# Seven block products for eight in q, k and v: pre-norm attention and a top-1 adapter with projections through DRAM and a list-scheduled order

## The chip, the core and the metric

The kernel runs on one core of a Trainium2 chip. Times are device microseconds of one execution of the whole program. The engines are TensorE (PE; PEld is its weight load), VectorE (DVE), ScalarE (ACT), GpSimd (POOL) and SyncE (SP), which here issues every DMA.

## What is computed

Four sequences of 1024 tokens by 1024 features, all fp32. Each goes through attention with 32 heads of 32 features and rotary positions, and then through a layer that adds, for each token, the low-rank adapter (rank 16) of the one expert of eight that scores highest.

```
h = layernorm(x)
q, k, v = h @ wq, h @ wk, h @ wv          # 1024 x 1024 each
q, k = rotary(q), rotary(k)
p = softmax(causal(q @ k.T / sqrt(32)))   # per head
x = x + (p @ v) @ wo
h = layernorm(x)
gate = one_hot(argmax(h @ route.T)) * max(h @ route.T)
x = x + sum_e gate[e] * (h @ A[e].T) @ Bw[e].T
```

## The kernel before, in words

**Units.** The work is cut into 32 units: sequence b (0 to 3) and group g of four heads (0 to 7). A unit's q, k and v are 128 features by 1024 tokens each.

**Preparation.** A sequence's x is loaded in eight tiles of 128 tokens (`load_x`), normalized on DVE (`find_moments`, `normalize`), transposed on PE (`transposed`, L194) and kept as `xnT`, two halves of 512 tokens.

**Projections.** `chain` (L326) makes one of q, k, v for one half of the tokens: eight matmuls of 128x512 (L337) that accumulate in one PSUM bank. ACT evicts the bank; q and k are then rotated by a shuffle and a sine product on DVE (L369, L371) and a cosine product and a sum on POOL (L370, L375), and stay in SBUF as `qT` and `kT`. A unit has six chains, 48 matmuls. v is turned in 32x32 blocks (L1105), stored to DRAM and loaded in another layout (`spread_values`).

**Attention.** Queries go in 16 tiles of 64. `score_round` (L417) makes one to four tiles of scores in a four-bank PSUM tile, 16 matmuls of 32x32 weights per tile (L430). ACT copies them to SBUF (L441), POOL masks the diagonal (L444), DVE finds the maxima (`find_tops`, L462, joined over partitions at L483), ACT exponentiates (L491) and DVE turns the probabilities in 32x32 blocks (L516). `value_pieces` (L612) multiplies them by v for eight tiles at once: per step of 64 keys, eight matmuls of up to 256 columns (L634). `scale_values` divides by the sums on DVE (L654), straight out of PSUM, and the result goes to DRAM. Nine of the units' half-blocks get their reciprocal sums by a PE transpose (L605), the others through DRAM.

**Output.** `finish_steps` (L717) takes a tile of 128 tokens: the projection by wo (L751, 16 matmuls, wo streamed in chunks of 256 KB), the sum with x (L757), a second norm, its transposes, routing (L773) and adapter (L812), and the store. For the last sequence wo stays in SBUF, and the part of the projection that doesn't need the last unit is done ahead.

**What sets the order.** An order written out by hand: `SLOTS` lists the rounds of a unit; between the rounds, `fill` and `do_some` put steps from a list of dense work (projections of the next unit, output tiles of the sequence before), woven by `weave`, `change_steps` and step costs. All engines then run their instructions in this program order.

Of the kernel before, what the change touches and what calls it, by code (L numbers as in the profile page):

```python
# [24 lines left out]

SLOTS = (
    ((7, 0, 512), (6, 0, 448)),
    ((5, 0, 384), (4, 0, 320), (3, 0, 256)),
    "second",
    ((2, 0, 192), (1, 0, 128), (0, 0, 64), (9, 0, 640)),  # L30
    ((15, 0, 1024),),
    ((14, 0, 960),),
    ((13, 0, 896),),
    ((12, 0, 832),),
    "first",
    ((11, 0, 768), (8, 0, 256)),
    ((10, 0, 704), (8, 256, 576)),
)


SHARE, VALUE_SHARE, EACH = 3600, 2600, 330

APART_BY = 3

LENGTHS = (4.4, 4.3, 2.6, 3.0, 4.3, 3.8, 3.8, 3.8, 2.8, 2.8, 3.3)


class Step:


    def __init__(self, run, cost=1.0, chunk=None):
        self.run, self.cost, self.chunk = run, cost, chunk


def weave(main, other):

    if not other:  # L60
        return list(main)
    out, taken = [], 0
    for n, step in enumerate(main):
        out.append(step)
        due = (n + 1) * len(other) // len(main)
        out += other[taken:due]
        taken = due
    return out + list(other[taken:])
# [3 lines left out]
def tile_preln_attn_then_top1_lora(  # L72
# [25 lines left out]
    NC = D // P  # L98
    NT = S // P
# [8 lines left out]
    COUNT = {"row": 5, "w": 2, "qkT": 4, "rope": 3, "vT": 1, "vals": 1}  # L108
    small = ctx.enter_context(tc.tile_pool(name="small", bufs=2))
    dram = ctx.enter_context(tc.tile_pool(name="dram", bufs=2, space=bass.MemoryType.DRAM))  # L110
    ps_s = ctx.enter_context(tc.tile_pool(name="ps_s", bufs=1, space=bass.MemoryType.PSUM))
    ps = ctx.enter_context(tc.tile_pool(name="ps", bufs=4, space=bass.MemoryType.PSUM))
    ctx.enter_context(tc.manual_schedule())

    def bank(shape, name):
        return ps.tile(shape, F32, tag="ps", name=name)

    def row(name):
        return big.tile([P, D], F32, tag="row", name=name, bufs=COUNT["row"])


    eye_sb = const.tile([P, P], F32, name="eye_sb")

    def load_x(b, t, tag="row"):
        xr = big.tile([P, D], F32, tag=tag, name=f"x_{b}_{t}", bufs=COUNT[tag])
        nc.sync.dma_start(xr, x[b, t * P : (t + 1) * P, :])
        return xr

    def load_head(n, tag):
        wt = big.tile([P, NC, P], F32, tag=tag, name=f"w{n}_0", bufs=COUNT[tag])  # L130
        nc.sync.dma_start(wt, {"q": wq, "k": wk, "v": wv}[n][:, :P].rearrange("(c p) n -> p c n", p=P))
        return wt


    x_first = [load_x(0, 0)]
    nc.sync.dma_start(eye_sb, eye)
    x_first.append(load_x(0, 1))
    w_first = {"q": load_head("q", "w")}
    x_first.append(load_x(0, 2))
    w_first["k"] = load_head("k", "w")  # L140
    x_first.append(load_x(0, 3))
    rot_sb = big.tile([P, P], F32, tag="rope", name="rot_sb", bufs=3)
    nc.sync.dma_start(rot_sb, rot)
    cos_sb = const.tile([P, S], F32, name="cos_sb")
    nc.sync.dma_start(cos_sb, cos)
    sin_sb = const.tile([P, S], F32, name="sin_sb")
    nc.sync.dma_start(sin_sb, sin)
    w_first["v"] = load_head("v", "vals")


    causal_sb = const.tile([P, SQ], F32, name="causal_sb")
    for i in range(P // SQ):
        half, odd = divmod(i, 2)
        nc.sync.dma_start(
            causal_sb[i * SQ : (i + 1) * SQ],
            causal[half * SQ : (half + 1) * SQ, odd * SQ : (odd + 1) * SQ],
        )
    both_sb = const.tile([P, 2, SQ], F32, name="both_sb")
    first_sb = const.tile([P, E], F32, name="first_sb")
    nc.sync.dma_start(first_sb, first)  # L160
    half_sb = const.tile([P, 1], F32, name="half_sb")
    nc.vector.memset(half_sb, -0.5)
    sign_sb = const.tile([P, 1], F32, name="sign_sb")
    rec_sb = const.tile([P, 2, SQ], F32, name="rec_sb")
    nc.vector.memset(rec_sb, 0.0)

    def sign_sines():

        nc.vector.tensor_reduce(sign_sb, rot_sb, AX.X, ALU.add, negate=True)
        nc.vector.tensor_scalar(sin_sb, sin_sb, sign_sb, None, ALU.mult)  # L170
        of_eye = eye_sb.rearrange("p (s c k) -> p s c k", c=2, k=SQ)
        nc.vector.tensor_tensor(both_sb, of_eye[:, :, 0], of_eye[:, :, 1], ALU.add)


    def find_moments(src, name):
        stats = small.tile([P, D // 512, nc.vector.BN_STATS_DIM], F32, tag="stats", name=f"st_{name}")
        for i in range(D // 512):
            nc.vector.bn_stats(stats[:, i, :], src[:, i * 512 : (i + 1) * 512])  # L178
        mv = small.tile([P, nc.vector.BN_AGGR_DIM], F32, tag="mv", name=f"mv_{name}", bufs=3)
        nc.vector.bn_aggr(mv, stats)  # L180
        ve = small.tile([P, 1], F32, tag="ve", name=f"ve_{name}")
        nc.vector.tensor_scalar(ve, mv[:, 1:2], EPS, None, ALU.add)
        rstd = small.tile([P, 1], F32, tag="rstd", name=f"rstd_{name}", bufs=3)
        nc.gpsimd.tensor_tensor(rstd, ve, half_sb, ALU.pow)
        return mv, rstd

    def normalize(dst, src, moments):
        mv, rstd = moments
        nc.vector.tensor_scalar(dst, src, mv[:, 0:1], rstd, ALU.subtract, ALU.mult)

    def layernorm(dst, src, name):
        normalize(dst, src, find_moments(src, name))

    def transposed(dst, src, name, scalar_only=False):  # L194

        pts = []
        for half in range(NC // 4):
            pt = bank([P, 4, P], f"pt_{name}_{half}")
            for i in range(4):
                c = 4 * half + i  # L200
                nc.tensor.transpose(pt[:, i, :], src[:, c * P : (c + 1) * P], eye_sb)  # L201
            pts.append(pt)
        nc.scalar.copy(dst[:, 0:4, :], pts[0])  # L203
        if scalar_only:
            nc.scalar.copy(dst[:, 4:8, :], pts[1])
        else:
            nc.vector.tensor_copy(dst[:, 4:8, :], pts[1])


    units = [(b, g) for b in range(B) for g in range(NG)]  # L210
    weights = {(0, n): wt for n, wt in w_first.items()}
    to_load = deque((u, n) for u in range(1, len(units)) for n in "qkv")

    def load_weights():
        if not to_load:
            return
        u, n = to_load.popleft()
        g = units[u][1]
        wt = big.tile([P, NC, P], F32, tag="w", name=f"w{n}_{u}", bufs=2)
        w = {"q": wq, "k": wk, "v": wv}[n]  # L220
        nc.sync.dma_start(wt, w[:, g * P : (g + 1) * P].rearrange("(c p) n -> p c n", p=P))
        weights[u, n] = wt

    xnTs, qTs, kTs, vTs = {}, {}, {}, {}


    postponed = []

    def do_postponed(cost):
        for item in list(postponed):  # L230
            item[0] -= cost
            if item[0] <= 0:
                postponed.remove(item)
                item[1]()

    class Two:


        def __init__(self, parts):
            self.parts = parts  # L240

        def __getitem__(self, key):
            rows, cols = key
            k, at = divmod(cols.start, HALF)
            return self.parts[k][rows, at : at + cols.stop - cols.start]

    class Norm:

        def __init__(self, b, after, homes={}):
            self.b, self.after, self.homes = b, after, homes
            self.found = self.scaled = 0
            self.x, self.moments = {}, {}

        def load(self, *tiles):  # L260
            u = self.b * NG
            for t in tiles:
                n = self.homes.get(t)
                if not n:
                    self.x[t] = load_x(self.b, t)
                    continue
                if n == "chunk":
                    self.x[t] = Two([])
                    for cols in (slice(0, HALF), slice(HALF, D)):
                        part = big.tile([P, HALF], F32, tag="chunk", name=f"x_{self.b}_{t}", bufs=4)  # L270
                        nc.sync.dma_start(part, x[self.b, t * P : (t + 1) * P, cols])
                        self.x[t].parts.append(part)
                    continue
                dsts = qTs if n == "q" else kTs
                if u not in dsts:
                    dsts[u] = big.tile([P, S], F32, tag="qkT", name=f"{n}T_{u}", bufs=4)
# [49 lines left out]
    def chain(u, n, tb, parts=False):  # L326
# [6 lines left out]
        def step(c):  # L333
# [10 lines left out]
            if c == NC - 1:  # L344
                finish()
# [52 lines left out]

# [822 lines left out]
```

## Time and profile before

| | us |
|---|---|
| median of 3 runs (lowest, highest) | 2712.2 (2709.39, 2714.22) |
| span of the profiled execution | 2709.0 |
| PE busy | 2664.0 |
| DVE busy | 2143.4 |
| ACT busy | 1723.6 |
| POOL busy | 601.9 |

The span runs from the first to the last instruction of the profiled execution, and the times of the runs take in what lies around it: the median is 3.2 us above the span. A unit takes 64 to 66 us in the first sequence, where there is no output projection yet, and 81.5 us later (distance between the first of the score rounds with 512 columns).

### The profile page before, as it was taken

Reading aid. Unit: us, or ns where it says so; the run is one execution under the profiler, and the core shown is the slowest. Engines: PE = TensorE matmul, PEld = TensorE weight load, DVE = VectorE, ACT = ScalarE, POOL = GpSimd, SP = SyncE. Lnnn points to the kernel's source line nnn. Section 1 sums busy time; section 2 is a strip of 40 time slices with the busy share of each in tenths; the row PEclk is TensorE's granted clock in tenths of the full one; section 3 lists DMA queues with packets and bytes.
Section 4 is the critical chain, followed back from the end, with each engine's and each line's share of the span. In section 5 each row is a group of like instructions: output and inputs, shape, how many; then the busy total and the mean of one; then the engine's idle time right before and its main releaser. Section 6 shows DMA issues by size and latency. Waiting matters only on the chain.

```text
span 2709.0 us, 84062 instructions
## 1 busy us (share of the span) xinstructions
PE 2664.0 (98%) x35108; PEld 1300.3 (48%) x35108; DVE 2143.4 (79%) x4256; ACT 1723.6 (64%) x4978; POOL 601.9 (22%) x845
## 2 busy tenths in 40 slices
PE   8999999999999999999999999999999999999998
PEld 5444444444444544545444445444544444544445
DVE  4899988887787787887777877888787777787555
ACT  2878777876666676665666666766566666666521
POOL 2222222222222222222122222222212222212000
PEclk9999999999999999999999999999999999999999
DMA  3222323226554455652555554574355555446421
GB/s 119 60 72 73 76 72 80 64 65 176 139 141 130 124 138 154 165 164 65 164 158 134 136 132 131 137 189 140 83 158 143 154 134 138 122 132 198 127 70 53
DMA packets 465900, 332.74 MB, mean 123 GB/s; under 512 B 160880, under 2 KB 382320, under 8 KB 465520
## 3 DMA queue, kind: packets, MB, share of 16 engines
q1 hardware_dynamic: 465520, 327.37, 44.3%
q8 instruction: 276, 4.52, 0.7%
q14 instruction: 104, 0.85, 0.1%
HBM read 277.01 MB, written 50.26 MB: 121 GB/s over the span
## 4 chain that ended last, share of the span: by engine, by line
PE 80%; DVE 13%; ACT 3%; DMA 1%; issue 1%; POOL 1%; SPq 1%; POOLq 0%; DVEq 0%; ACTq 0%
PE po L751 15%; PE pq L337 14%; PE pk L337 14%; PE pv L337 12%; PE s L430 11%; PE av L634 8%; DVE top L462 4%; DVE pr L516 4%; PE ph L773 2%; PE pf L812 2%; ACT pr L491 1%; DVE both L483 1%; ACT pr L441 1%; PE pt_f L201 1%; DVE st_a L178 1%
## 5 line engine op out<-in xcount | busy, mean ns | idle before, releaser
L491 ACT ACTIVATE pr<-pr,both 128x256 f32<-128x256 f32 (+15 forms) x2048 | 1044.4, 518 | 53.6 <-DVE both L483 53.6
L441 ACT COPY pr<-s 128x640 f32<-128x640 f32 (+14 forms) x544 | 525.2, 1017 | 660.2 <-PE s L430 659.6
L462 DVE TENSOR_REDUCE top<-pr 128x2 f32<-128x960 f32 (+15 forms) x768 | 650.7, 894 | 251.4 <-POOL pr L444 250.8
L516 DVE STREAM_TRANSPOSE pr<-pr 128x1024 f32<-128x1024 f32 (+11 forms) x768 | 664.7, 908 | 34.1 <-ACT pr L491 30.7
L444 POOL TENSOR_TENSOR pr<-pr,causal_sb 128x128 f32<-128x128 f32 x512 | 237.2, 470 | 1158.3 <-ACT pr L441 1149.8
L337 PE MATMUL pv<-xnT,wv 128*128 128x512 f32 x1024 | 486.3, 602 | 0.0
L337 PE MATMUL pq<-xnT,wq 128*128 128x512 f32 x1008 | 478.1, 602 | 0.2 <-ACT xnT L203 0.2
L337 PE MATMUL pk<-xnT,wk 128*128 128x512 f32 x1008 | 477.1, 602 | 0.4 <-ACT rawq L363 0.4
L430 PE MATMUL s<-kT,qT 32*32 32x256 f32 (+4 forms) x17408 | 394.0, 386 | 9.4 <-POOL pr L444 3.2
L491 ACT ACTIVATION_READ_ACCUMULATOR pr<-pr,both 128x1 f32 x2048 | 400.8, 196 | 0.0
L751 PE MATMUL po<-chunk,attn 128*128 128x512 f32 x736 | 380.0, 602 | 2.5 <-DMA chunk<-in_wo 2.5
L430 PEld LDWEIGHTS s<-kT,qT 32*32 32x32 f32 x17408 | 187.3, 103 | 267.5 <-issue 100.7
L337 PEld LDWEIGHTS pk<-xnT,wk 128*128 128x128 f32 x1008 | 181.2, 190 | 235.7 <-issue 234.5
L337 PEld LDWEIGHTS pq<-xnT,wq 128*128 128x128 f32 x1008 | 183.2, 191 | 226.8 <-issue 225.0
L337 PEld LDWEIGHTS pv<-xnT,wv 128*128 128x128 f32 x1024 | 185.6, 190 | 218.1 <-issue 216.6
L634 PE MATMUL av<-pr,vals 64*32 64x256 f32 (+3 forms) x12288 | 272.8, 319 | 4.2 <-DVE pr L516 4.1
L634 PEld LDWEIGHTS av<-pr,vals 64*32 64x32 f32 x12288 | 213.0, 106 | 112.7 <-issue 66.1
L483 DVE TENSOR_TENSOR both<-top 32x4 f32<-32x4 f32 (+3 forms) x1152 | 207.4, 180 | 23.8
L751 PEld LDWEIGHTS po<-chunk,attn 128*128 128x128 f32 x736 | 135.6, 190 | 167.2 <-issue 149.4
L654 DVE TENSOR_TENSOR at<-av,by 128x256 f32<-128x256 f32 x128 | 48.2, 418 | 107.2 <-PE av L634 60.4
L751 PE MATMUL po<-wo,attn 128*128 128x512 f32 x256 | 116.6, 596 | 0.0
L375 POOL TENSOR_TENSOR qT<-qT,swapq 128x512 f32<-128x512 f32 x64 | 82.5, 1289 | 141.4 <-DVE swapq L371 141.4
(89 smaller groups left out, 1558.4 us busy)
## 6 DMA issues: line engine op xcount, KB each, us to landing
chunk<-in_wo SPq DMA_DIRECT2D x368, 256.0 KB, 3.8
vals<-vd SPq DMA_DIRECT2D x256, 128.0 KB, 4.3
x<-in_x SPq DMA_DIRECT2D x56, 512.0 KB, 5.4
wq<-in_wq SPq DMA_DIRECT2D x32, 512.0 KB, 4.7
wk<-in_wk SPq DMA_DIRECT2D x32, 512.0 KB, 4.0
wv<-in_wv SPq DMA_DIRECT2D x32, 512.0 KB, 4.3
vd<-vT SPq DMA_DIRECT2D x128, 128.0 KB, 4.6
out_y<-x SPq DMA_DIRECT2D x32, 512.0 KB, 2.6
```

The source lines that it names most:

```text
L337: nc.tensor.matmul(at["p"], lhsT=wt[:, c, :], rhs=xnTs[b, tb][:, c, :], start=(c == 0), stop=(c == NC - 1),)
L375: nc.gpsimd.tensor_tensor(dst[:, cols], dst[:, cols], other, ALU.add)
L430: nc.tensor.matmul(sc[i * SQ : (i + 1) * SQ, h, at : at + w].rearrange("p (j k) -> p j k", k=SQ), lhsT=of_q[rows, 2 * t + half], rhs=of_k[ ...
L441: nc.scalar.copy(pr[:, :, k0 : k0 + w], sc[:, :, at : at + w])
L444: nc.gpsimd.tensor_tensor(diagonal, diagonal, causal_sb.unsqueeze(1).to_broadcast([P, HG, SQ]), ALU.add)
L462: nc.vector.tensor_reduce(top[:, k, h : h + step], places[u, t][:, h : h + step, :], AX.X, ALU.max, negate=True,)
L483: nc.vector.tensor_tensor(dst[rows], src[rows], src[other], op)
L491: nc.scalar.activation(pr[:, h, :], pr[:, h, :], AF.Exp, bias=tops[u, t][:, h : h + 1], accum_out=dens[u, t // QT][:, t % QT, h : h + 1],)
L516: nc.vector.transpose(pr, pr)
L634: nc.tensor.matmul(avs[half][h * HD : (h + 1) * HD, t0:, :], lhsT=v[rows, j, h * HD : (h + 1) * HD], rhs=rhs, start=(j == 0), stop=(j == n ...
L751: nc.tensor.matmul(st["po"], lhsT=lhsT, rhs=rhs, start=(c == start), stop=(c == stop))
L773: nc.tensor.matmul(ph, lhsT=st["ynT"][:, c, :], rhs=w[:, c - i * RA, :], start=(c == 0), stop=(c == NC - 1),)
```

## The change

The kernel is written anew around the same parts. What differs:

- **Products.** Two outputs are made together (q and k of one group; v of two groups). The normalized x is seen as blocks A11 to A22 (512 tokens by 512 features) and the two weight slices as B11 to B22. Seven products of four matmuls each take the place of eight (`group`), with sums of blocks of x (S1 to S4) and of weights (T1 to T4) as operands, and sums of the results on DVE, POOL and in PSUM. The first group of all (q, k of unit 0) is made in the plain way.
- **Where things lie.** The T blocks are made once, in the first sequence, and stored in DRAM (`combine`), later loaded (`fetch_blocks`). q and k go to DRAM after their rotation (`rotate`), v after its turning (`spread`), and attention loads them. The next sequence's x is prepared during this one: blocks and S sums are written to DRAM (`prepare`) and fetched at the change of sequence (`fetch_sequence`).
- **Attention by quads.** Rounds are one tile each for 15 to 8, then (7, 6), (5, 4), (3, 2, 1, 0). Probabilities are multiplied by v for four tiles at once (`apply_quad`, up to 128 columns); ACT evicts the result, POOL divides (`finish_block`).
- **Output.** `finish_tile` does the same steps; the last sequence's tiles start only when all of its units are done.
- **Order.** Each piece is a `Task` with an engine, a length, a position and predecessors. `Plan.order` runs a list schedule over these lengths (the free engine takes the ready task with the lowest position whose buffers are free), and the program is written in order of the planned starts.

```diff
-SLOTS = (
-    ((7, 0, 512), (6, 0, 448)),
...
+ROUNDS = ((15,), (14,), (13,), (12,), (11,), (10,), (9,), (8,), (7, 6), (5, 4), (3, 2, 1, 0))
...
+SIGNAL = {"PE": 0.35, "ACT": 0.3, "DVE": 0.3, "POOL": 0.3}
+DENSE = 0.859
...
+    def group(b, kind, g, pos, w):
...
+        p1 = product("A11", "B11", one, True, [], True)
+        s1 = copy_out(r1, one, factor, pos, p1, True)
+        p2 = product("A12", "B21", two, True, [p1], True)
...
+        c11 = add(
+            "DVE", 0.62, lambda: add_bank(r1, two, factor), pos - 100, [p2, s1], [r1, two]
+        )
+        outs[0, 0] = r1, c11
+        p6 = product("S2", "T2", one, False, [p2, s1])
+        s2 = copy_out(r2, one, 1.0, pos, p6, True)
+        p5 = product("S1", "T1", two2, True, [p6], True)
+        s5 = copy_out(r5, two2, 1.0, pos, p5, True)
+        p7 = product("S3", "T3", one, False, [p5, s2])
+        s3 = copy_out(r3, one, 1.0, pos, p7, True)
+        c22 = add(
+            "POOL",
...
+            lambda: nc.gpsimd.tensor_tensor(r3.tile, r3.tile, r5.tile, ALU.add),
...
+        p3 = product("S4", "B22", two2, False, [p7, s5])
...
+        p4 = product("A22", "T4", one, False, [p3, s3])
+        c21 = copy_out(r4, one, factor, pos, p4, True)
...
+    def rotate(u, which, tb, raw, pos, t):
...
+            nc.sync.dma_start(store[u][:, cols], raw.tile)
...
+    def attend(b, g):
...
+            lambda: nc.sync.dma_start(kt.tile, k_dram[u]),
...
+            [stored["k", u, 0], stored["k", u, 1]],
...
+    def apply_quad(u, quad, pos, pr, vt, loads, turned, of_blk):
...
+        nj = QUADS * (quad + 1)
...
+                                [of_h.ap[0], [pitch(quad), QUADS - t0], [1, SQ]],
...
+            nc.scalar.copy(dst, src)
...
+            nc.gpsimd.tensor_tensor(done.tile, done.tile, by.tile, ALU.mult)
...
+    for t in plan.order():
+        for buf in t.opens:
+            make(buf)
+        t.run()
```

## Prediction

> **What bounds the kernel now.** I read the page's busy times first, then the chain that ended last, then busy times by stretch, then the timeline of TensorE inside one stretch.
>
> ```profile
> PE 2664.0 (98%) x35108; PEld 1300.3 (48%) x35108; DVE 2143.4 (79%) x4256; ACT 1723.6 (64%) x4978; POOL 601.9 (22%) x845
> ```
> ```profile
> PE 80%; DVE 13%; ACT 3%; DMA 1%; issue 1%; POOL 1%; SPq 1%; POOLq 0%; DVEq 0%; ACTq 0%
> ```
> TensorE (PE) is idle for 45.0 of 2709.0 us, and 80% of the chain is its work. So what the change takes off PE counts in full, unless another engine or a wait comes up to it. The next engine is VectorE (DVE). Busy times by stretch (columns: stretch and length; PE, weight loads, DVE, ACT, POOL busy; granted clock; DMA share; GB/s):
>
> ```profile
> 0.00:60.00 60.00, 50.03 (x250) 34.57 (x251) 28.48 (x57) 12.93 (x22) 15.42 (x20) 1.00 0.43 134
> 60.00:150.00 90.00, 87.34 (x1326) 40.99 (x1326) 72.25 (x138) 64.64 (x192) 23.25 (x34) 0.98 0.22 53
> 150.00:600.00 450.00, 439.33 (x6885) 207.51 (x6873) 405.95 (x802) 357.76 (x1033) 121.66 (x171) 1.00 0.30 74
> 600.00:2400.00 1800.00, 1791.60 (x23730) 866.63 (x23727) 1437.34 (x2850) 1160.11 (x3367) 407.20 (x564) 1.00 0.52 140
> 2400.00:2487.00 87.00, 87.00 (x1129) 41.49 (x1128) 67.96 (x138) 57.10 (x164) 18.65 (x26) 1.00 0.47 129
> 2487.00:2709.00 222.00, 208.70 (x1846) 109.09 (x1817) 131.44 (x275) 71.08 (x201) 15.75 (x31) 1.00 0.33 103
> ```
> The reader is to see two regimes. In the first sequence (150 to 600) there is no output projection yet, DVE is busy 405.95 of 450 us (90%), and PE still idles only 10.7 us (2.4%). From 600 to 2400 DVE is at 80% and PE idles 8.4 us (0.5%). The granted clock is full almost throughout. Prices on PE come from its timeline (start, length, records; a step's price is the distance to the next start):
>
> ```profile
> 699.96 1.88 PE L337 MATMUL pk<-xnT,wk 128*128 128x512 f32 x4
> 701.68 1.02 PE L751 MATMUL po<-chunk,attn 128*128 128x512 f32 x2
> 702.53 1.88 PE L337 MATMUL pq<-xnT,wq 128*128 128x512 f32 x4
> ...
> 764.55 3.69 PE L634 MATMUL av<-pr,vals 64*32 64x256 f32 x128
> 768.16 2.84 PE L337 MATMUL pk<-xnT,wk 128*128 128x512 f32 x6
> 770.93 2.35 PE L634 MATMUL av<-pr,vals 64*32 64x256 f32 x128
> 773.22 1.12 PE L751 MATMUL po<-chunk,attn 128*128 128x512 f32 x2
> ...
> 778.70 1.91 PE L430 MATMUL s<-kT,qT 32*32 32x96 f32 x128
> 780.54 1.13 PE L751 MATMUL po<-chunk,attn 128*128 128x512 f32 x2
> ```
> One fp32 matmul is two records. From 699.96 to 702.53 there are three of 128x512: 0.857 us each.
>
> **The change, part by part (PE).**
>
> *Projections.* The program built from the changed kernel has 1,316 matmuls of 128x512 for q, k, v and 128 of 128x128 (first group, like 32 whole ones): 1,348, against 1,520 + 64/4 = 1,536 before. 188 x 0.857 = **-161 us**. That is certain as work: these matmuls lie on the chain (q, k, v are 14 + 14 + 12% of it).
>
> *Probabilities times values.* Before, a unit (four heads) has one piece of eight steps at 256 columns, 768.16 - 764.55 = 3.61 us, and two ramps from 256 to 32 columns, 2.29 us each: 8.19. After, the columns are the same but in quads: 24 steps of 128 columns and four ramps 128, 96, 64, 32. A step of 128 columns at half of 3.61/8 is 0.226; a quad ramp is the end of the old ramp, 2.29 less its first four steps (0.451 + 0.395 + 0.338 + 0.282) = 0.82. 24 x 0.226 + 4 x 0.82 = 8.70, and some 0.3 for three more entries: 9.0, +0.85 a unit, x 32 = **+27 us**. From below 0 (same columns). From above by the record rate of narrow tiles: the timeline has 128 records of narrow score tiles in 1.84 us, 14.4 ns each; three-tile rounds run at 16.5 ns (96 records in 1.58 us); 640 records x 16.5 = 10.6 us a unit: +76.
>
> On these narrow steps the rows show 14.4 ns per record, 29 ns per fp32 matmul. The Trainium skill ("TensorE: Matmul & The Clock Gate", section "Wait — 56ns, not 53.3ns?") says that start-to-start "never drops below ≈25 ns however small N is", which speaks against cutting the steps narrower. Taken per record, this would be an estimated 640 x 25 = 16 us a unit, +250 us in all, and the change would lose. The row contradicts that reading already (14.4 ns), and taken per fp32 matmul the rule asks 320 x 25 = 8 us, below what I price.
>
> *Scores.* Tile 8 is no longer split in two and each of the tiles 8 to 15 is a round by itself. The lone rounds fall by 0.05 us per 32 columns from 1.07 (512) to 0.92 (416); continued, 384, 352, 320 and 288 cost 0.87, 0.82, 0.77, 0.72. Against the mixed rounds of before (1.43, 1.43, 1.58, 1.84 in the timeline), I get -0.23 a unit, **-7 us** (bounds -15 to +10). The 36 transposes of sums (L605) go, at 0.93 us per eight as pt_f has them: **-4 us**. Switches between dense and narrow work cost PE as before: its order has 2,450 rows of equal instructions against 2,504. Sum of PE work: -161 + 27 - 7 - 4 = **-145 us** (bounds -180 to -79).
>
> **The other engines, which decide how much of it arrives.**
>
> *DVE.* Added: 94 sums out of PSUM at 0.685 (L757: 50.7 us for 74) = 64; two more rounds of joins a unit, 256 x 0.163 (L483) = 42; v turned in 128 pieces at 0.401 (L516, 128x256) = 51 in place of 38 (L1105); 24 block sums of the first sequence at 0.70 = 17. Removed: scaling at L654, 48, and copies at L207, 17. Net +71: 2214 us. About 123 of them fall into the last 222 us (131 before), so some 2,091 stand before those. *ACT*: 128 more evictions of 256 columns at 0.378 (L441) = 48, 47 more of 512 at 0.58 = 27, 28 transposed halves = 16, less a little: some 1,810 us. *POOL*: 64 + 47 + 48 + 40 new operations of 128x512 at 1.28 (L370): +250, 850 us. Neither comes near PE's 2,530; both are hidden beside it, and would cost their +86 and +250 only if PE had nothing else to do meanwhile.
>
> *DVE beside POOL.* The same sine product takes 0.69 us in the timeline where POOL rests and 814 ns in the mean:
>
> ```profile
> L371 DVE TENSOR_TENSOR swapk<-swapk,sin_sb 128x512 f32<-128x512 f32 x64 | 52.1, 814 | 2.2
> ```
> So 250 us more of POOL can stretch DVE. From below nothing (the two rarely meet), from above 18% of its tensor-tensor work; I take 2 to 4% of the whole.
>
> *DMA.* q and k go out and come back (+67 MB), combined weights are stored and reloaded (+42), the next sequence's blocks are written and fetched (+44): 327 becomes some 480 MB.
>
> ```profile
> q1 hardware_dynamic: 465520, 327.37, 44.3%
> ```
> By bytes that is 44.3% x 480/327 = 65% of the queues, less by packets, since the 128-byte pieces of v go. The mean bandwidth is hidden. The danger is order: SP issues 2,094 DMAs in one queue (1,627 before). New waits on it: a unit's k and q are loaded only when its group has been rotated on DVE and POOL and stored. Queued behind such a store or load stand weights, wo chunks and values, and PE's next group waits for those.
>
> **PE's waiting.** Now 45 us: 10 in the first 60, 2.7 to 150, 10.7 + 8.4 in the middle, 13.3 in the last 222. After: the start waits for DVE (51 us of norms, rotations and block sums before the first score's maximum, against some 40 us of PE): +8. The tail is eight whole tiles of 16 x 0.857 + 0.93 + 1.85 + 0.16 + 1.72 = 18.4 us behind a last unit of some 60, plus an end chain of 15: 222 us again, with a thinner last unit: +5. In the middle, DVE's 2,091 us in about 2,380 are 88%, near the 90% of the first sequence, where PE lost 2.4%. I take 2% of 2,330 = 47 where it is some 20 now: +27. Together **+40** (bounds -10, every wait hidden better, to +130, the first regime's loss doubled and the start's too).
>
> Sum: 2709 - 145 + 40 = 2604 on the profiled execution's span of 2709.0; the median of the runs is 3 us above that span: **2607 us**.
>
> **Rivals.**
> - *All of it arrives.* Projections of later units can run ahead, since q, k, v lie in DRAM, so PE always has something. For it: the 0.5% of 600 to 2400. Against it: DVE at 88% rather than 80%. 2709 - 145 + 3 = 2567.
> - *DVE becomes the bound.* It is stretched 6% by POOL (2,091 becomes 2,216) and fills at most the 91% it reached from 150 to 450 (136.7 and 136.4 us of two stretches of 150): 2,216/0.91 = 2,436, and 222 for the tail: 2658, with the 3: 2661. For it: 814 against 690 ns. Against it: transposes and reductions, most of DVE's work, stretch less.
> - *Slower: one landing exposed per group.* 47 groups of seven products each fetch their operands (seven, or four in the first sequence) through the one queue. If a late store ahead of them exposes one landing, 4 us (chunks and weights land in 3.8 to 4.7 us by the median of their issues), this is 47 x 4 = 188: 2567 + 188 = 2755. It decides from 145/47 = 3.1 us a group. For it: SP already waits 572 us in front of wo chunks behind PE. Against it: six weight buffers, some 20 us of PE work ahead.
> - *It doesn't do what it says.* Excluded for the products (the counts above); it could be that the projections are not what PE waits on, but PE is the chain.
>
> **How the numbers follow.** Forecast 2607 (2575 to 2640): 0.45. All arrives, 2567: 0.2. DVE bound, 2661: 0.17. Slower, 2755: 0.15; the remaining 0.03 lies about no change (0.2%, what a measurement can tell, is 5 us). Faster 0.82, same 0.03, slower 0.15. The range takes in the first three and the edge of no change, and leaves most of the slower case and a little below: 2552 to 2710.
>
> **What would show it.** Right: PE busy near 2,530 us at 97%, DVE near 2,210 to 2,280, 88% before the tail; 128-column steps of probabilities times values at 0.23 us; idle of PE spread, mostly behind DVE or ACT. Wrong: PE waiting for weight buffers or for k and q by DMA (slower rival); DVE over 91% in the middle with a sine product over 850 ns (DVE bound); value steps near 0.4 us; a long hole at the start or between sequences, which I priced at a few us.

## The result and the profile after

| | before | after |
|---|---|---|
| median (lowest to highest) | 2711.9 us (2709.4 to 2714.2) | 2829.4 us (2819.6 to 2838.8) |
| ratio, 95% interval | 1 | **1.0435** [1.0409, 1.046] |
| span of the profiled execution | 2709.0 | 2817.8 |
| PE busy; idle (span less busy) | 2664.0; 45.0 | 2598.9; 218.9 |
| mean granted clock | 0.998 | 0.976 |

The changed kernel is 4.35% slower. Forecast were 2607 us, 2552 to 2710. The page after, its busy times and its chain:

```profile
span 2817.8 us, 99968 instructions
...
PE 2598.9 (92%) x41960; PEld 1294.6 (46%) x41960; DVE 2281.6 (81%) x4570; ACT 1805.8 (64%) x5136; POOL 889.1 (32%) x1035
...
q1 hardware_dynamic: 398048, 477.62, 55.1%
q8 instruction: 329, 5.39, 0.8%
...
PE 45%; DVE 13%; issue 4%; ACT 1%; DMA 1%; POOL 0%; SPq 0%; POOLq 0%; DVEq 0%; ACTq 0%
```
The work went mostly as planned: PE's busy time fell by 65 us although its clock was lower. The other side is idle time, +174: -65 + 174 = +109, the whole change of the span. So the question is not what the products cost but why PE stands still. PE's waits after (columns: us in total, times, longest), and the one row put down to "issue" before:

```profile
PE av L1118 <- issue: 100.3, 52, 5.4
PE av L1118 <- DVE pr L1083: 32.5, 30, 4.1
PE s L967 <- issue: 19.5, 23, 2.5
PE s L967 <- ACT pr L998: 11.6, 12, 1.9
```
```profile
PE s L430 <- issue: 2.5, 2, 1.3
```
The largest cause is "issue": PE waits for nothing that the profile shows. Of the +174, "issue" makes +122, waits for DVE +39 and for ACT +15. Waits put down to DMA come to 1.9 us (wo and the adapter's weights); none is for k, q or v. Where the "issue" gaps lie is told by PE's timeline (start, length, records, the idle time before):

```profile
708.18 1.82 PE L1118 MATMUL av<-pr,val 64*32 64x128 f32 x128
709.93 1.12 PE L762 MATMUL pc_qk<-S,b_qk 128*128 128x512 f32 x2
...
752.47 2.98 PE L1118 MATMUL av<-pr,val 64*32 64x128 f32 x169
756.53 1.30 PE L1118 MATMUL av<-pr,val 64*32 64x128 f32 x87 [1.08 <-issue]
...
826.15 2.62 PE L1118 MATMUL av<-pr,val 64*32 64x128 f32 x169
831.50 2.17 PE L1118 MATMUL av<-pr,val 64*32 64x128 f32 x87 [2.73 <-issue]
```
Eight key steps (708.18 to 709.93) take 1.75 us, about as priced (1.81). But runs of 16 steps, 256 records, break off in the middle, between equal instructions whose operands were all there. Counted from the program's start, these breaks are multiples of some 127.5 records apart (127, 128, 255, 383, 510, 638 ...). A record is one weight load and one matmul, so 128 are 256 PE instructions; the instruction queue q8 moved 5.39 MB in 329 packets, 5.39/329 = 16 KB each, which for 256 instructions is 64 bytes an instruction. **PE has used up its block of instructions before the next one is there.** All breaks in the middle of a run, of values and of scores, sum to 107 us; before there were 2.5.

The trace's DMA records show the blocks themselves. PE's 84,311 instructions after (weight loads, matmuls and its sequencer's) are 329.3 blocks of 256, and q8 moved 329 packets; before, 70,694 are 276.1, and q8 moved 276. All 68 breaks end 1.14 to 1.62 us behind the landing of such a packet. "Issue" gaps that end this way sum to 113 us; the other 12 us are six gaps at the first record of a value run, with no packet landing in the 14 us before, and what ended those isn't shown. In 16 of the 68 breaks the packet set out only after PE had stopped, up to 1.9 us after; what held it back stays open.

The second thing to see is the clock, here behind such gaps (same stretch, the same eight records of 128x512 twice):

```profile
849.96 0.71 PE L967 MATMUL s<-k,q 32*32 32x64 f32 x36 [1.15 <-issue]
850.60 5.95 PE L762 MATMUL pa_qk<-S,T_qk 128*128 128x512 f32 x8
856.39 3.60 PE L762 MATMUL pc_qk<-S,T_qk 128*128 128x512 f32 x8
```
Right after two gaps (1.95 us for ACT at 847, 1.15 here) the eight take 5.95 us instead of 3.60. Around the gap of 2.73 us at 831 (shown above) the granted clock (third number from the right) falls to half (columns: stretch and length; PE, weight loads, DVE, ACT, POOL busy; clock; DMA share; GB/s):

```profile
827.00:831.20 4.20, 1.77 (x127) 1.52 (x110) 4.01 (x11) 2.57 (x10) 0.14 (x1) 1.00 0.91 262
831.30:834.60 3.30, 3.10 (x88) 2.53 (x88) 3.27 (x8) 0.37 (x1) 0.89 (x1) 0.50 0.07 14
834.70:838.00 3.30, 3.30 (x70) 1.50 (x69) 1.30 (x2) 0.49 (x1) 0.79 (x1) 1.00 0.20 63
```
Most low stretches are 3.4 us long, so that each loses 1.7 us, and most stand behind a gap of 2 us or more. Summed over the span, (1 - granted clock) x length is **66.6 us** after and 5.1 before; PE was at work in 56 and 5 of them. So PE's work at full clock is 2598.9 - 56 = 2543 against 2664.0 - 5 = 2659: **-116**. The budget: -116 of work, +51 of clock, +174 of waiting: +109.

### The profile page after: what moved, and what is told of

Its sections match the earlier page's. It is cut to its first block, busy times and chain, and to the rows that moved or that the text cites. A ratio compares the mean times of both kernels' runs of the same rounds, so it can differ in the third digit from the quotient of the medians.

```text
span 2817.8 us, 99968 instructions
## 1 busy us (share of the span) xinstructions
PE 2598.9 (92%) x41960; PEld 1294.6 (46%) x41960; DVE 2281.6 (81%) x4570; ACT 1805.8 (64%) x5136; POOL 889.1 (32%) x1035
## 3 DMA queue, kind: packets, MB, share of 16 engines
q1 hardware_dynamic: 398048, 477.62, 55.1%
q8 instruction: 329, 5.39, 0.8%
## 4 chain that ended last, share of the span: by engine, by line
PE 45%; DVE 13%; issue 4%; ACT 1%; DMA 1%; POOL 0%; SPq 0%; POOLq 0%; DVEq 0%; ACTq 0%
PE po L1305 12%; PE av L1118 7%; PE s L967 6%; PE pa_qk L762 5%; DVE top L1026 5%; PE pa_v L762 3%; PE pc_qk L762 3%; DVE pr L1083 3%; DVE both L879 2%; PE ph L1366 2%; PE pf L1434 2%; PE pc_v L762 2%; PE pb_qk L762 2%; PE pt_f L351 1%; PE pb_v L762 1%
## 5 line engine op out<-in xcount | busy, mean ns | idle before, releaser
L1059 ACT ACTIVATE pr<-pr,both 128x512 f32<-128x512 f32 (+15 forms) x2048 | 1045.1, 518 | 110.5 <-DVE both L879 110.0
L1026 DVE TENSOR_REDUCE top<-pr 128x2 f32<-128x1024 f32 (+15 forms) x768 | 655.7, 895 | 157.5 <-POOL pr L1004 155.1
L998 ACT COPY pr<-s 128x2048 f32<-128x2048 f32 (+15 forms) x512 | 530.0, 1067 | 287.8 <-PE s L967 280.0
L1083 DVE STREAM_TRANSPOSE pr<-pr 128x640 f32<-128x640 f32 (+11 forms) x768 | 666.6, 907 | 58.3 <-ACT pr L1059 53.4
L1305 PE MATMUL po<-wo,attn 128*128 128x512 f32 x1024 | 503.8, 616 | 6.6 <-issue 5.0
L1118 PE MATMUL av<-pr,val 64*32 64x128 f32 x20480 | 328.8, 267 | 137.1 <-issue 100.3
L967 PE MATMUL s<-k,q 32*32 32x512 f32 (+3 forms) x16384 | 395.3, 402 | 32.4 <-issue 19.5
L1118 PEld LDWEIGHTS av<-pr,val 64*32 64x32 f32 x20480 | 297.4, 109 | 249.5 <-issue 171.1
L879 DVE TENSOR_TENSOR both<-top 32x4 f32<-32x4 f32 (+2 forms) x1408 | 312.5, 222 | 28.2
L762 PE MATMUL pa_qk<-A,T_qk 128*128 128x512 f32 x440 | 212.0, 607 | 0.4 <-ACT r_qk L730 0.4
```

The costliest lines, as they stand in the source:

```text
L762: nc.tensor.matmul(at.tile, lhsT=buf.tile[:, c, :], rhs=act.tile[:, c, :], start=first_ and c == 0, stop=c == KC - 1, skip_group_check=not ...
L879: nc.vector.tensor_tensor(dst[r], src[r], src[o], op)
L967: nc.tensor.matmul(s.tile[i * SQ : (i + 1) * SQ, h, at : at + w].rearrange("p (j k) -> p j k", k=SQ), lhsT=of_q[r, 2 * (t % QUADS) + half] ...
L998: nc.scalar.copy(place(t), s.tile[:, :, at : at + w])
L1026: nc.vector.tensor_reduce(got["top"][:, k, h : h + step], place(t)[:, h : h + step, :], AX.X, ALU.max, negate=True,)
L1059: nc.scalar.activation(pr[:, h, :], pr[:, h, :], AF.Exp, bias=got["both"][:, k, h : h + 1], accum_out=den(blk)[:, t % 8, h : h + 1],)
```

## The experiments

Two theories. **F**: blocks of instructions come too slowly for runs of narrow matmuls, and this and the low clock behind the pauses make the loss. **D**: probabilities are late, because DVE has more to do than planned. For the kernels that follow, "pauses" are gaps put down to "issue" in the middle of a value or score run, "clock" is the sum above over the whole span, pauses included; "before" ran beside all of them at 2710.5 to 2713.1 us.

| kernel | us | ratio [95%] | PE busy | idle | pauses | clock |
|---|---|---|---|---|---|---|
| after | 2829.4 | 1.0435 [1.0409, 1.046] | 2598.9 | 219 | 107 | 67 |
| half the values (1) | 2699.4 | 0.9958 [0.9943, 0.9973] | 2556.1 | 137 | 11 | 65 |
| before, quads (2) | 2830.1 | 1.0445 [1.0429, 1.046] | 2710.8 | 117 | 79 | 18 |
| before, traffic (3) | 2744.9 | 1.0126 [1.0111, 1.0141] | 2673.9 | 68 | 1 | 12 |
| both (4) | 2880.6 | 1.0625 [1.0607, 1.0643] | 2731.6 | 149 | 83 | 37 |
| eighth product (6) | 2949.5 | 1.0887 [1.0853, 1.0921] | 2753.3 | 208 | 99 | 66 |
| planner's lengths (7) | 2867.1 | 1.0579 [1.0563, 1.0595] | 2601.4 | 261 | 94 | 107 |
| spread (8) | 2936.9 | 1.0844 [1.0825, 1.0862] | 2649.4 | 282 | 17 | 131 |
| gentle (9) | 2790.3 | 1.0288 [1.0267, 1.031] | 2599.7 | 188 | 47 | 63 |
| rests (10) | 2786.7 | 1.0275 [1.0256, 1.0294] | 2598.8 | 190 | 48 | 59 |
| longer (11) | 2844.4 | 1.0481 [1.0459, 1.0503] | 2604.7 | 238 | 33 | 97 |
| one join, half the values (12) | 2610.4 | 0.9617 [0.9601, 0.9633] | 2533.2 | 83 | 4 | 43 |
| one join (13) | 2751.7 | 1.0152 [1.0137, 1.0167] | 2583.0 | 174 | 101 | 55 |
| rests, copies on DVE (14) | 2704.8 | 0.9972 [0.996, 0.9983] | 2579.0 | 122 | 32 | 29 |
| **rests, copies on POOL (15)** | **2666.9** | **0.9828** [0.9811, 0.9844] | 2576.8 | 95 | 43 | 34 |
| copies on POOL alone (16) | 2762.1 | 1.0185 [1.0164, 1.0207] | 2583.3 | 175 | 110 | 58 |
| before, copies on DVE (17) | 2695.6 | 0.9939 [0.9924, 0.9954] | 2660.9 | 33 | 0 | 3 |
| before, copies on POOL (18) | 2699.5 | 0.9954 [0.9939, 0.9969] | 2660.0 | 41 | 4 | 2 |

### F: what the pauses are

**1. Half the values.** In `apply_quad` of the changed kernel:

```diff
-                    for half in range(2):
+                    for half in range(2 if j == 0 else 1):
...
-                            stop=(j == nj - 1),
+                            stop=(j == nj - 1 or half == 1),
```


> The changed kernel, in which the second half of the queries gets only the first key step of probabilities times values (it leaves out nearly half of these matmuls; each step still streams 128 columns, so PE's streaming time stays). Theory F (PE runs out of instructions: it is refilled in blocks of 256 and stands still at a block's end): the pauses inside value runs go, some 100 us of PE idle, and the granted clock rises from 0.976 towards 0.99; 2690 to 2730 us. Rival D (an order planned on too short DVE lengths, so PE waits for DVE and ACT): same as the changed kernel within 30 us, 2800 to 2830.

2699.4 us, 130 less than after, of which only 40 are work at full clock. The pauses fall from 107 to 11 us. So most of what the runs of narrow matmuls cost is not their work. The clock did not recover (65), though F had expected that it would; waits of 33 us for DVE's transposes (33 before the edit) and 22 for ACT's copies (12) left gaps that lower it.

**2. The value edit in the kernel before.** Eight-tile steps of up to 256 columns cut into two of up to 128 (scalings doubled for it), nothing else of the change:

```diff
-                for h in range(HG):
-                    for half in range(2):
...
+                for lo, hi in ((t0, QT // 2), (max(t0, QT // 2), QT)):
...
+                    for h in range(HG):
+                        for half in range(2):
```


> The kernel before with one part of the change alone: each step of probabilities times values in two matmuls of up to 128 columns instead of one of 256 (and two narrow scalings more per half). F: pauses inside value runs appear in a kernel that had none, at distances of whole blocks of 256 instructions; idle +40 to +120 us, 2770 to 2850 us. Rival W (quads cost only their width and entries, as priced): 2735 to 2750, no pauses. D says nothing of it: 2712 to 2750.

2830.1: this edit alone costs +4.45%, as much as the whole change. PE's waits now begin with a line that the kernel before did not have:

```profile
PE av L640 <- issue: 76.9, 52, 3.3
PE pt_a L201 <- DVE x L189: 8.9, 2, 7.7
PE av L640 <- DVE pr L516: 6.3, 7, 2.7
```
All 76.9 us lie in the middle of runs, at the same distances as after, in a kernel without products of seven and without a planner, and all its 55 pauses (scores included) end 1.23 to 1.64 us behind the landing of a q8 packet. PE's busy time rose by 47 us, of which 12 are clock: the value steps were priced at +27.

**3 and 4. Traffic.** 488 copies of 256 KB from DRAM to DRAM, one behind each chunk load, in the kernel before (3) and together with the value edit (4):

```diff
+    def spare_copy():
+        k = copies[0] % 8
+        copies[0] += 1
+        sink = dram.tile([P, 512], F32, tag="sink", name=f"sink_{copies[0]}", bufs=8)
+        nc.sync.dma_start(sink, wo[k * P : (k + 1) * P, :512])
...
+        spare_copy()
```


> The kernel before with a copy from DRAM to DRAM of 256 KB behind each chunk load (488 copies, about 125 MB, near the traffic that the change adds); no other work. If a busier DMA makes the refill slower (theory T beside F): pauses on PE appear in value and score runs, 2725 to 2790 us. If traffic as such is harmless: 2707 to 2720.

> The kernel before with both the value steps by 128 columns and the added copies in DRAM, that is, two earlier edits together. If the pauses at block ends depend only on how fast the instructions are used up, the two costs add: some 2865 us, with pauses of about 1.5 us on average as with the value edit alone. If the traffic makes the fetching of blocks slower as well, the pauses grow and the time is 2880 to 2930 us.

(3) costs 33 us and has no pauses (1 us): its time lies in the range of slower fetching, but for another reason, waits for wo chunks, which grow from 2.5 to 28 us. (4) is 2880.6 where the two costs add to 2864, at the edge of the same theory's range; but its 52 pauses in value runs sum to 79.7 us, 1.53 each against 1.48. Traffic of this kind does not make the fetching slower; 12 of the 17 us that (4) has beyond the sum are clock (37 against 18 + 7). With 455 MB moved in (4) and 477.62 in the changed kernel, traffic is an unlikely cause of its pauses, though the added copies run from DRAM to DRAM and the kernel's own do not.

**5. Bursts.** The disputed cost by itself: ahead of the kernel before, five bursts over constants.

```diff
+        for n in (32, 64, 128, 256, 512):
...
+            for i in range(128):
+                for h in range(4):
+                    for half in range(2):
+                        r = slice(half * 64, (half + 1) * 64)
+                        nc.tensor.matmul(
+                            outs[half][h * 32 : (h + 1) * 32, :n],
+                            lhsT=cos_sb[r, h * 32 : (h + 1) * 32],
+                            rhs=cos_sb[r, :n],
```


> The kernel before with five bursts of 1024 matmuls each put ahead of its work, over constants, in the same eight positions as the value steps but 32, 64, 128, 256 and 512 columns wide, and 16 matmuls of 128x512 before each burst; it computes the same besides. F: a block of 256 instructions takes a fixed time to come, so that 128 records of the 32-, 64- and 128-column bursts all take about 3.3 us on average (the value edit alone: 1.8 us of work and 1.5 of pause), with pauses at every 128th record; the 512-column burst, some 7 us per 128 records, has none. If the pauses belong to the value steps' own operands and not to the fetching, no burst has pauses and the time of 128 records goes with the columns.

One run, 3120.0 us. The timeline of PE in the bursts of 32, 64, 128 and 256 columns, then the stretches of the first three (granted clock third from the right):

```profile
42.18 1.53 PE L170 MATMUL burst<-cos_sb 64*32 64x32 f32 x128 [1.92 <-issue]
45.63 1.53 PE L170 MATMUL burst<-cos_sb 64*32 64x32 f32 x128 [1.92 <-issue]
...
105.55 1.47 PE L170 MATMUL burst<-cos_sb 64*32 64x64 f32 x128 [1.76 <-issue]
...
112.73 2.04 PE L170 MATMUL burst<-cos_sb 64*32 64x64 f32 x128 [1.41 <-issue]
116.18 2.04 PE L170 MATMUL burst<-cos_sb 64*32 64x64 f32 x128 [1.41 <-issue]
...
171.65 3.76 PE L170 MATMUL burst<-cos_sb 64*32 64x128 f32 x255
177.01 2.02 PE L170 MATMUL burst<-cos_sb 64*32 64x128 f32 x128 [1.59 <-issue]
180.46 2.02 PE L170 MATMUL burst<-cos_sb 64*32 64x128 f32 x128 [1.44 <-issue]
...
241.41 56.48 PE L170 MATMUL burst<-cos_sb 64*32 64x256 f32 x2048
```
```profile
36.10:90.60 54.50, 26.40 (x1788) 21.84 (x1775) 0.00 (x0) 0.00 (x0) 0.00 (x0) 0.50 0.02 5
107.80:158.90 51.10, 30.43 (x1764) 26.10 (x1764) 0.00 (x0) 0.00 (x0) 0.00 (x0) 0.50 0.02 4
159.00:241.00 82.00, 58.37 (x2110) 39.49 (x2108) 0.00 (x0) 0.00 (x0) 0.00 (x0) 1.00 0.01 3
```
The clearest view of the study: starts are 3.45 us apart whatever the width (45.63 - 42.18, 116.18 - 112.73, 180.46 - 177.01), work and pause always summing to that, with a pause at each 128th record; some periods are 0.3 or 0.55 longer. The period is the same at half clock (nearly all of the bursts of 32 and 64 columns) and at full clock (128). In the trace's DMA records all 45 pauses end 1.25 to 1.54 us behind the landing of a q8 packet. **A block of 256 PE instructions comes in 3.45 us**, 27 ns a record. At 256 columns 128 records take 56.48/16 = 3.53 us, and no pause is left. A burst begins with 159 to 255 records before its first pause, so that one to two blocks are at hand after 15 us of dense work. That is why eight value steps in a row (128 records in 1.75 us) pass and sixteen do not.

The Trainium skill ("Runtime: NRT & Kernel Launch", section "Instruction fetch mechanics") has the block of 16 KiB and 256 instructions, and says that crossing its boundary is "mostly hidden". These rows agree with the block and not with the second: it is hidden only behind work of 3.45 us a block. The page gives PE room for 2048 instructions; the bursts ran dry after 510 at most.

**6. The eighth product.** In `group`, `p2` made twice:

```diff
+        p2 = product("A12", "B21", two, False, [p2])
```


> The changed kernel with the product p2 done twice, so that eight products are computed again instead of seven: nothing but TensorE work is added, some 161 us of it by the row of the 128x512 matmul; the output is not the reference's. If TensorE's own work still sets the time, as the fetch theory F has it, the eighth product costs close to its price: 2940 to 3000 us. If the time is set by another engine or by waits for the probabilities (theory D), the dense work fills holes and costs far less: 2840 to 2920 us.

+120 us in the median and +144 between the two spans, +154 of PE's busy time. So dense work does not sink into the holes: what the seven products save (161 as priced) arrives, to about three quarters or more.

**7. The planner's lengths.** Lengths as measured, same instructions:

```diff
-    return 0.09 + 0.00103 * n
+    return 0.05 + 0.00114 * n
...
-            joined = add("DVE", 0.66, join, pos - 20, reduced)
+            joined = add("DVE", 0.9 if n == 1 else 1.0, join, pos - 20, reduced)
```


> The changed kernel with the lengths that the planner gives VectorE's, ScalarE's and GpSimd's steps set to the ones that the profile after shows (the joins 0.9 and 1.0, a VectorE elementwise step 0.05 + 0.00114 per element, a GpSimd one 0.25 + 0.0021 per element, and so on); the same instructions in another order. If late probabilities, planned too early, make much of the loss (D), the idle time behind VectorE and ScalarE falls and the time with it: 2730 to 2800 us. If the pauses at the ends of instruction blocks and the low clock behind them make it (F), little changes: 2800 to 2840 us.

Neither: 38 us slower than after, with more waiting for DVE (64 us in 14 long gaps at the values) and a lower clock. A list schedule with truer lengths is not a better one; it cleared nothing up.

**8 to 11. Spacing.** Value runs in pieces that a list schedule holds back for a while after the last piece: pieces of four steps and score rounds too, 1.7 us (8); pieces of eight, only the second of a run held for 1.7 us (9); every piece, behind score rounds too (10); the second held for 3.4 us (11). The core of (9):

```diff
+                        if item[2].yields and now < hold - 1e-9:
+                            late = late or item
+                            held.append(item)
+                            continue
...
+            last.rest, last.yields = 1.7, i > 0
```


> The changed kernel with value runs cut into pieces of 4 steps (128 instructions on PE) and a list schedule that, after such a piece or a round of scores, takes dense matmuls for 1.7 us if any is ready. Same work. F: blocks are used up more slowly, most pauses go; 2700 to 2770 us. D: attention comes later, nothing is won: 2815 to 2860.

> The changed kernel with value runs as before in pieces of 8 key steps, but with the second piece of a run started only 1.7 us after the first, so that dense matmuls come between. F: fewer blocks of 256 instructions are used up within 2 us, the pauses in the middle of value runs fall from some 89 us to under half of it, and the time to 2760 to 2810 us. D: the attention comes later and the waits grow: 2830 to 2880 us.

> The changed kernel with value runs in pieces of 8 key steps, where every piece starts only when 1.7 us of other TensorE work lie behind the last piece or score round. F: the pauses in the middle of value runs, 30 us with the gentler edit, fall under 20 and the time to 2760 to 2790 us. D: the attention comes later, the waits for probabilities and the low clock take back what the pauses give: 2790 to 2850 us.

> The changed kernel with the second piece of a value run held back for 3.4 us of other work instead of 1.7. If the pauses that are left are those of two pieces still too close, the time falls to 2760 to 2785 us; if they come from pieces beside score rounds, it stays at 2785 to 2810 us.

(9) did what F expected: pauses 107 to 47, time -39 us. (10) gave no more; its pauses at the values stayed at 30 us, where under 20 was expected. (8) and (11) lie above both of their expected ranges. (8) took nearly all pauses away and lost 108 us: held score rounds make attention late, idle time goes to waits for ACT (64 us) and DVE (58), and the clock falls. (11) shows the same on a small scale: pauses 33, waits for DVE 56 and for ACT 40. The "issue" gaps behind which no packet landed, nearly all at the first record of a value run, also grow: from 12 us after to 35 in (9), 37 in (10) and 57 in (8). So in this order the pauses can be exchanged for waits for the probabilities, and there D comes in.

### D: late probabilities

The joins of the maxima (L879) are four minima over 32 partitions with the halves crossed. Before and after, the groups of one tile (count, us, mean ns):

```profile
L483 DVE TENSOR_TENSOR both<-top 32x4 f32<-32x4 f32 x640 | 104.4, 163 | 12.7
```
```profile
L879 DVE TENSOR_TENSOR both<-top 32x4 f32<-32x4 f32 x1024 | 216.7, 212 | 20.9
```
All joins together went from 207.4 us to 312.5 (+105; priced +42), and 110 us of ACT's idle time wait for them (53.6 before).

**12 and 13. One join.** One copy over 128 partitions in their place, which leaves the pairing of the two halves of a row out; with half the values as in (1), and alone:

```diff
-                with_other(got["both"], got["top"], ALU.min)
+                nc.vector.tensor_copy(got["both"], got["top"])
```


> The kernel with half of the values left out, and the joins of the maxima as one copy over 128 partitions instead of four 32-partition minima, so that both halves of a row keep their own maximum and some 250 us of VectorE work are left out as well. If what was left of the loss there (131 us of idle TensorE, 66 of low clock) came mostly from late probabilities, both fall by a third to a half and the time to 2600 to 2650 us, about where the forecast for the whole change lay; if VectorE's work is not what is late, it stays within 2670 to 2700 us.

> The changed kernel with the joins of the maxima as one copy over 128 partitions (both halves of a row keep their own maximum, so the pairing is left out), all values kept. If late probabilities cost by themselves, about the 89 us that the same edit took from the kernel with half the values: 2730 to 2760 us. If earlier probabilities only make value runs denser, so that the pauses at block ends grow by as much, 2780 to 2830 us.

(12) lands at 2610.4, 89 us below (1); (13) takes 78 us from the changed kernel. D is right as well, and the two causes are separate: in (13) the pauses are what they were (101). With both gone, in (12), PE idles 83 us, and the time is about the forecast; that is a coincidence, since (12) leaves out 49 us of PE's work at full clock that the changed kernel, and the forecast, have in them.

**14 to 18. Fewer joins, all computed.** A softmax allows any shift that both halves of a row share. The maximum over the even key blocks does for these inputs (not for all: a score in an odd block can lie far above it, and its exponential then grows without bound): two copies, on DVE (14) or on POOL (15), beside the rests of (10); on POOL without the rests (16); and in the kernel before, on DVE (17) and POOL (18).

```diff
-                got["both"] = small.tile(
...
-                with_other(got["both"], got["top"], ALU.min)
+                got["both"] = got["top"]
+                for i in (0, 2):
+                    nc.gpsimd.tensor_copy(
+                        got["top"][(i + 1) * SQ : (i + 2) * SQ], got["top"][i * SQ : (i + 1) * SQ]
+                    )
```


> The kernel with rests for the fetching (2787 us) with another shift in the softmax that needs less VectorE work: both halves of a row take the maximum over the even key blocks, so that two copies over 32 partitions do where four minima stood; all is computed. The joins fall from some 310 us to 150. D: time falls by a third to two thirds of those 89 us: 2720 to 2765 us. If VectorE isn't late any more in that order: 2775 to 2795 us.

> As the run with two copies on VectorE, but the two copies on GpSimd, so that VectorE has no joins at all (some 310 us less). If VectorE's load is what makes probabilities late: 2690 to 2740 us, at or under the kernel before. If the way over another engine and GpSimd's own queue (masks, the rotary products) cost as much as they save: 2760 to 2830 us.

> The changed kernel with the maxima shared by two copies on GpSimd, as in the run at 2667 us, but without the rests between value pieces; all is computed. If the two causes add, the rests are worth about the 43 us that they gave alone and the copies the rest: some 2705 to 2725 us, with some 100 us of pauses in the middle of runs. If the copies do it all: 2665 to 2690 us.

> The kernel before with the same other shift: two copies on VectorE in place of four minima, about 100 us less VectorE work. TensorE is busy 98% there and waits some 4 us for probabilities in all, so nothing to gain: 2700 to 2715 us. If VectorE held back the kernel before as well, it falls under 2690 us.

> The kernel before with the maxima shared by two copies on GpSimd; all is computed. Two copies on VectorE took 15 us from it. If what helped was that VectorE has less to do, 2685 to 2697 us; the changed kernel with copies and rests (2667 us) stays ahead by 20 to 30 us. If the way over GpSimd is late in an order written out by hand, 2700 to 2740 us.

(14) is 82 us below (10) and (15) **2666.9**, 1.72% under the kernel before [0.9811, 0.9844]; both lie below the ranges expected of them. Its page and PE's waits:

```profile
PE 2576.8 (96%) x41960; PEld 1268.6 (47%) x41960; DVE 1985.6 (74%) x3162; ACT 1805.4 (68%) x5136; POOL 1020.6 (38%) x1739
...
PE 83%; issue 2%; DVE 2%; ACT 2%; POOL 1%; DMA 1%; SPq 0%; POOLq 0%; ACTq 0%
```
```profile
PE av L1134 <- issue: 26.0, 20, 3.5
PE s L981 <- issue: 18.1, 18, 2.1
PE av L1134 <- DVE pr L1099: 12.2, 8, 7.0
```
TensorE is the chain again (45% to 83%), DVE has 313 us less than in (10), and the waits for its transposes are 12 us.

The two edits help each other. The copies alone give 67 us (16), the rests alone 43 (10), both 162; (16) at 2762 is above both times expected of it. With (16) the pauses are all there (110), with (15) 43. The reading that fits all rows, argued and not shown by itself: a rest costs nothing only while the probabilities are early enough to wait. In its favour: the 37 us of "issue" gaps without a packet in (10) are 0 in (15).

The kernel before gains 15 us from two copies on DVE (17), between the two times expected: its idle time went from 45 to 33. On POOL it gains 11 (18). Against its better one, (15) is ahead by 29 us.

## Why the prediction was wrong

- **The work**: -145 forecast, -116 found at full clock, inside the bounds. By the trace's records, each counted from the end of the one before it and at full clock, q, k and v gave -154 (forecast -161), the values +36 (+27; the same edit in (2) gave +35), the scores -5 (-7), the output projection +9 (0) and the sums' transposes -5 (-4). The price of a step, 0.226 us, was right (eight in 1.75); runs pay more.
- **PE's waiting**, "Together +40 (bounds -10 ... to +130)": this step failed; it was +174. All but 13 us of it was derived from DVE's load ("I take 2% of 2,330 = 47"). It had no place for a wait that the rows of before hardly show (2.5 us): 107 us of pauses at the ends of instruction blocks. The waits that it did think of, for DVE and ACT, grew by 54 us, not far from its +40. Before, a run at full width took 3.61 us for 128 records (3.45 is the limit) and a ramp 2.29, and these short runs lived on the block at hand. Halving the columns at an equal count of columns doubled the instructions per microsecond; the prediction counted 640 records a unit and priced them by their rate, never by their delivery.
- **The clock** had no term; it cost 51 in PE's busy time. The full clock of before was taken over though idle time was forecast to grow.
- **DVE**: 2214 forecast, 2282 found, at the upper end of the named span (2,280). Of +68, joins are 63 ("256 x 0.163"): the older ones became longer as well, for the reason in the last section. The busy share, 81%, is far below the 91% of the rival; yet joins and transposes were late, and one copy in the joins' place took 78 us off the time (13). That fits delay on the way to the values better than the engine's fill, but (13) takes away both and does not separate them.
- **Traffic**: 477.62 MB at 55.1% for 480 at 65%. "One landing exposed per group", the slower rival, named the right side by the wrong mechanism: PE waits only 1.9 us for operands by DMA.
- **The narrow-matmul rule** of the Trainium skill that is set aside there, 25 ns from start to start: taken per record it asked for 250 us more. Records without a pause take 11.5 ns (64 columns, 1.47 us for 128) to 15.8 (128 columns, 2.02) at full clock in the bursts, so the rows were read rightly. But delivery puts 27 ns per record under any longer run.
- "All of it arrives" was right for the products by about three quarters or more (6); with both causes gone and half the values left out, 2610 (12) is still above its 2567.

## What to carry to other kernels

Count instructions per microsecond, not only columns: where a run of matmuls uses up more than one or two blocks of 256 instructions faster than they come, the runs have to be spaced by dense work or made of wider matmuls. Dense work can stand between only if the narrow work's operands are early, so shorten the chain that prepares them first. And an engine at 81% can hold the end back when its short steps lie between two others.

## What was not expected of the hardware

- A block of 256 TensorE instructions (128 weight loads and 128 matmuls) arrives in 3.45 us in runs of 32, 64 and 128 columns, at half and at full clock, and heavier traffic (455 MB in place of 327) left the pauses at 1.5 us on average.
- The bursts of 64 columns fell to half clock with pauses of 1.41 us in 3.45, and those of 128 columns kept the full clock with pauses of 1.44 to 1.99. So 128 records of 64 columns took 2.04 us, as many as of 128 columns (2.02), but 1.47 before the clock fell.
- Gaps of some 2 us can be enough for a low clock: behind 25 of the changed kernel's 33 gaps of 2 us or more, and 3 of its 21 of 1.5 to 2, a stretch at half clock begins during the gap or within 3.5 us of its end. The Trainium skill ("TensorE: Matmul & The Clock Gate", section "What's actually happening") puts the fall behind an idle window of some 3.4 us; here it also stands behind single gaps as short as 2.23 us (at 1220 us of the changed kernel's profile).
- The minima over 32 partitions (32x4) have a median of 155 ns and a longest of 1265 after; the mean rose from 163 to 212 where POOL is busier (889 us for 602). The trace shows why: of all 1408 joins 186 took over 300 ns, and each of them ran beside a POOL instruction; nine in ten ended 12 to 26 ns after one ended. Above 160 ns each, these slow ones cost 91 us (39 of them and 26 us before), about the +63 that the price of the joins missed.
